# Cross attention with an adapter on one core: the adapter's sums over its heads as additions of halves, and the last rows stored in halves of columns

## The chip, the cores and the metric

The kernel runs on one core of a Trainium2 chip, everything in float32. The metric is the device time of one execution in microseconds (us). Five engines work beside each other: TensorE (PE, matrix products), VectorE (DVE), ScalarE (ACT), GpSimd (POOL) and SyncE (SP, which issues most of the DMAs, in order). Each has its own queue of instructions, and semaphores join them.

## The reference, cut to what matters

Two sequences of 2048 rows with 640 features attend to 124 text tokens, in 8 heads of 80. The last 4 tokens of the context feed an adapter: it forms 384 queries from them, attends with these to the 2048 rows of the sequence, multiplies by `Wq`, and attends again to its own 4 tokens. The 384 result rows are spread over the 2048 rows by an index, added to the text attention, and the sum goes through `Wout`.

```python
hs = _mha(query, keyt, valt)                     # text attention
ca_q1 = jnp.einsum('btc,th->bch', ca, Wq_ca)     # 384 adapter queries
ca_q1 = ca_q1[:, indices, :]                     # read for 2048 rows
ca_hs1 = _mha(ca_q1, residual, residual)         # attention to the rows of x
ca_hs2 = _mha(ca_hs1 @ Wq, ca @ Wk_ca, ca @ Wv_ca)
out = (hs + ca_hs2) @ Wout + b_out + residual
```

## The kernel before

The kernel is not one loop. Python generators describe pieces of work (`adapter`, `softmax`, `text_out_fast`, ...), each yields a `Do` for an engine with what it waits for, and a planner (`Desk`) simulates the engines: it adds up estimated durations (`desk.spent`) and issues next what is ready first, by rank among equals. The order found so is the program's order on each engine. L236 (VectorE, ScalarE and GpSimd work), L211 (products), L221 (transposes) and L256 (DMAs by SP) are the helpers through which all instructions go, so a profile names them all by these lines and the tiles tell them apart.

The adapter works on each sequence (batch `b`) in turn. Its weighted sums over the rows of x are never formed with 640 features; products with the keys of its second attention are carried along in their place. `contract(b, j, acc, at)` adds them up on PE in `acc` for two halves `j` of the eight heads, turns the result (`pt_acc`) and divides it, on DVE, into the tile `prod`. `prod` has shape (128 partitions, 3 groups of adapter queries, 2 halves `j`, 4 heads `g` in a half, 24), and the 24 are 8 heads of the second attention by 3 differences of tokens. `second(b)` then sums over the 8 heads of the first attention (`j` and `g`) into the scores `s2f`, in the function `less`, which goes on to take the maximum and subtract it. An exponential on ACT follows, `share` divides on DVE into `p2pad`, PE turns it (`pt_p`), and products with `w2_sb` give 384 rows that go to DRAM (`o`). From there `add_second` gathers rows on POOL by the index `query` and adds them to rows of output, by indirect DMAs.

The text attention goes in 16 units of two tiles of 128 rows. For unit `m`, `text_out_fast` takes probabilities that were turned by way of DRAM (`kept`, then `pT`), forms the heads' output (`ph`, `hs`), and multiplies by `Wout` in four chains with seven products for eight blocks; each chain's partial sum in PSUM (`po`) is added on DVE to a quarter of the output, half of a tile's 640 columns, in the residual's rows (`x_more` or `last_rows`, two sets of four row tiles). Each tile `(m, i)` receives four such additions, counted in `tile_left`; at the fourth `stored(m, i, ...)` issues the store on SP. In all units but the last, and there too if `o` were late, the gather comes between additions and store (`gather_last`); in the last it is done ahead of the additions.

The end of a chain's step, before:

```python
tile_left[m, i] = tile_left.get((m, i), 4) - 1
ends.setdefault((m, i), []).append(op.at)
if not tile_left[m, i]:
    yield Fork(stored(m, i, ends[m, i]), 1)
```

Of the kernel before, what the change touches and what calls it, by code (L numbers as in the profile page):

```python
# [11 lines left out]
ALU = mybir.AluOpType  # L12
AX = mybir.AxisListType

P = 128
# [49 lines left out]
class Desk:  # L65
# [188 lines left out]
    def dma(self, out, in_, us, issue=0.45, more=2.8):  # L254

        self.pin(self.nc.sync.dma_start(out, in_))  # L256
        self.spent += issue
        self.channel = max(self.channel, self.now + self.spent) + us
        self.landed = self.channel + more
# [3 lines left out]
def kernel(  # L263
# [20 lines left out]
    NCC = CAD // P  # L284
    NST = S // P
    NSB = S // 512
    HALF = H // 2
    SCALE = float(D) ** -0.5
    NUM, DEN = CAD - 1, S - 1
    T1 = T - 1  # L290
# [8 lines left out]
    UNITS = B * NST // 2  # L299
# [4 lines left out]
    desk = Desk(tc)  # L304
    matmul, transpose, copy, dma = desk.matmul, desk.transpose, desk.copy, desk.dma
# [13 lines left out]
    ending, late = Room(1), {}  # L319
# [47 lines left out]
    s2f = const.tile([P, NCC, HEADS, T], F32, name="s2f")  # L367
# [37 lines left out]
    for name, bands in (  # L405
# [4 lines left out]
        for n, (pattern, width, base, factor) in enumerate(bands):  # L410
            m = const.tile([P] + [k for _, k in pattern], F32, name=f"band_{name}_{n}")
# [1273 lines left out]
    def second(b):  # L1685

        def clear():
            desk.g_memset(p2pad, 0.0)
            desk.g_memset(p2pad[:, :, N2 : N2 + 1], 1.0)

        op = yield Do("POOL", clear, [])
        cleared = op.at
        N = NCC * HEADS
        s2 = s2f.rearrange("p a h t -> p (a h) t")
        p2 = small.tile([P, N, T], F32, tag="p2", name=f"p2_{b}", bufs=1)
        r2 = small.tile([P, N], F32, tag="r2", name=f"r2_{b}", bufs=1)

        def less():
            for ct in range(NCC):
                desk.v_tensor_reduce(  # L1700
                    s2f[:, ct, :, 1:],
                    late["prod"][:, ct, :, :, :].rearrange("p j g (h t) -> p h t (j g)", t=T1),
                    AX.X, ALU.add,
                )
            m2 = small.tile([P, N], F32, tag="m2", name=f"m2_{b}", bufs=1)
            desk.v_tensor_reduce(m2, s2, AX.X, ALU.max)
            desk.v_tensor_tensor(p2, s2, m2.unsqueeze(2).to_broadcast([P, N, T]), ALU.subtract)

        yield Do("DVE", less, [("prod", b, 0), ("prod", b, 1)])
        yield Do("ACT", lambda: desk.a_activation(p2, p2, AF.Exp, scale=SCALE))  # L1710

        def share():
            desk.v_tensor_reduce(r2, p2, AX.X, ALU.add)
            desk.v_reciprocal(r2, r2)
            p2of = p2.rearrange("p (a g j) t -> p a g j t", a=NCC, j=2)
            r2of = r2.rearrange("p (a g j x) -> p a g j x", a=NCC, j=2, x=1)
            for j in range(2):
                k0 = 2 * T * b + T * j
                desk.v_tensor_tensor(
                    p2pad[:, :, : 4 * G].rearrange("p a (g k) -> p a g k", g=4)[:, :, :, k0 : k0 + T],  # L1720
                    p2of[:, :, :, j, :], r2of[:, :, :, j, :].to_broadcast([P, NCC, 4, T]), ALU.mult,
                )

        op = yield Do("DVE", share)

        def turn(s):
            pt = bank(s[0], f"pt_p2_{b}")
            for ct in range(NCC):
                transpose(pt[: N2 + 1, ct * P : (ct + 1) * P], p2pad[:, ct, : N2 + 1], ident)
            return pt  # L1730

        op = yield Do("PE", turn, [op.at, cleared], needs=[(banks, 1)])
        pt, s = op.value, op.slots[0][0]

        def out_of(e):
            t = ea_tile(e[0], f"p2T_{b}")[: N2 + 1, 0, :]
            copy(t, pt[: N2 + 1, :CAD])
            return t

        op = yield Do("ACT", out_of, needs=[(eas, 1)], frees=[(banks, s)])  # L1740
        p2T, i = op.value, op.slots[0][0]
        here = op.at
        o2_of[b] = hbm.tile([CAD, H], F32, tag=f"o2_{b}", name=f"o2_{b}")
        for ct in range(NCC):
            op = yield Do("NONE", lambda e: ea_tile(e[0], f"o2_{b}_{ct}"), [here], needs=[(eas, 1)])
            o2, k = op.value.rearrange("p g k -> p (g k)")[:, :H], op.slots[0][0]
            for u in range(2):
                cols = slice(u * HALF, (u + 1) * HALF)

                def product(s, u=u, cols=cols):  # L1750
                    po = bank(s[0], f"po2_{b}_{ct}_{u}")
                    matmul(
                        po[:, :HALF], p2T[:, ct * P : (ct + 1) * P], w2_sb[:, cols],
                        start=True, stop=True,
                    )
                    return po

                op = yield Do("PE", product, [here, ("w2", u)], needs=[(banks, 1)])
                op = yield Do(
                    "ACT", lambda po=op.value, cols=cols: copy(o2[:, cols], po[:, :HALF]),  # L1760
                    frees=[(banks, op.slots[0][0])], marks=[("o2 part", b, ct, u)],
                )
            yield Do(
                "SP", lambda: dma(o2_of[b][ct * P : (ct + 1) * P, :], o2, 1.3),
                [("o2 part", b, ct, 0), ("o2 part", b, ct, 1)], frees=[(eas, k)],
                marks=[("o2 out", b, ct)],
            )
        yield Do(
            "NONE", lambda: None, [("o2 out", b, ct) for ct in range(NCC)], frees=[(eas, i)],
            marks=[("o2", b)],  # L1770
        )
        if b == B - 1:

            def more():
                sq_stack.close()
                late["ps"] = ctx.enter_context(tc.tile_pool(name="ps_r", bufs=1, space=bass.MemoryType.PSUM))
                banks.at += [desk.now] * 4
                ending.at += [desk.now] * 3

            yield Do("NONE", more, [])  # L1780
# [6 lines left out]
    kept_of, xr_of, gather_last, scored = {}, {}, {}, {}  # L1787

    def tiles(m):

        b, m = divmod(m, NST // 2)
        return [(b, 2 * m + k) for k in range(2)]
# [254 lines left out]
    def text_out_fast(m, rank):  # L2047
# [3 lines left out]
        for c0, n in ((0, 2), (2, 2), (4, 1)):  # L2051

            def product(s, z=None, c0=c0, n=n):
# [4 lines left out]
            op = yield Do(  # L2058
                "PE", product, [("pT", m), "v done"], needs=[(banks, 1)] + ([(hss, 1)] if c0 == 0 else []),
                frees=[(pTs, room_of["pT", m])] if c0 == 4 else [],  # L2060
                mode=(P, 32), rank=rank,
            )
# [9 lines left out]
        a = [[hs[:, 2 * k : 2 * k + 2, i * P : (i + 1) * P] for k in range(2)] for i in range(2)]  # L2072
# [29 lines left out]
        def chain(n, steps):  # L2102

            po, s, at = None, None, []
            for k, ((x, y, plus), after, ((i, u),)) in enumerate(steps):

                def product(s=None, k=k, x=x, y=y, plus=plus):
                    to = bank(s[0], f"po_{m}_{n}") if s else po
                    pairs = [(x[:, c], y[:, c]) for c in range(2)] if x is not None else []
                    if plus:  # L2110
                        pairs.append((last[plus[0]], five[plus[1]]))
                    for c, (l, r) in enumerate(pairs):
                        matmul(
                            to[:, :HALF], l, r, start=(k == 0 and c == 0), stop=(c == len(pairs) - 1),
                            skip_group_check=True,
                        )
                    return to

                op = yield Do(
                    "PE", product, after + at + ready, needs=[(banks, 1)] if k == 0 else [], mode=(P, P), rank=rank  # L2120
                )
                if k == 0:
                    po, s = op.value, op.slots[0][0]
                end = k == len(steps) - 1
                if end:
                    left["products"] -= 1
                    if not left["products"]:
                        hss.at[at_hs] = op.at.t

                def add(i=i, u=u, po=po):  # L2130
                    t = xr_of[m][i][0][:, u * HALF : (u + 1) * HALF]
                    desk.v_tensor_tensor(t, t, po[:, :HALF], ALU.add)

                op = yield Do("DVE", add, [op.at], frees=[(banks, s)] if end else [], rank=1)
                at = [op.at]
                tile_left[m, i] = tile_left.get((m, i), 4) - 1
                ends.setdefault((m, i), []).append(op.at)
                if not tile_left[m, i]:
                    yield Fork(stored(m, i, ends[m, i]), 1)
# [1 line left out]
        for n, steps in enumerate(chains):  # L2141
            yield Fork(chain(n, steps), 30 + m)

    fast_of, tile_left, ends = {}, {}, {}

    def added(m, k, u, po, s, at):

# [107 lines left out]
```

## Time and profile before

| what | us |
|---|---|
| median of three runs | 602.8 |
| lowest and highest | 601.7, 605.3 |
| profiled execution, its own time | 600.98 |
| span in its profile | 599.3 |
| reductions to `s2f`, first of batch 0 and of batch 1, start | 285.67, 476.77 |
| last addition on DVE, start | 594.92 |

The span runs from the first to the last instruction, the own time also holds what lies around it. Times in the profile are counted from the span's start. The page gives each engine's busy time, the chain of work that ended last, and the costliest groups of instructions. A row of the timeline gives start, duration, engine, helper line, operation, the tile written and those read with their shapes, and in brackets how long the engine had been idle and what ended that. The granted TensorE clock is full (1.000) throughout.

### The profile page before, as it was taken

The numbers are of one execution on the slowest core, as the hardware profiler recorded it, in microseconds if no ns is written. First come the engines' busy times: TensorE is split into PE (matmuls) and PEld (weight loads), VectorE is DVE, ScalarE is ACT, GpSimd is POOL, SyncE is SP. The second block draws the span as 40 slices with busy tenths as digits, with TensorE's granted clock in tenths as the row PEclk, the third lists the DMA queues.
The fourth block names the chain that finished last, engine by engine and source line by source line (L and its number), as shares of the span: only waits on it lengthen the run. The fifth ranks groups of instructions, "written<-read, shape, count | busy, mean of one in ns | idle before, by whom it ended". The sixth has DMA issues, their size and how long they took to land.

```text
span 599.3 us, 11936 instructions
## 1 busy us (share of the span) xinstructions
PE 583.7 (97%) x4535; PEld 363.9 (61%) x4535; DVE 390.8 (65%) x629; ACT 323.2 (54%) x913; POOL 133.4 (22%) x195
## 2 busy tenths in 40 slices
PE   9999999999999999999999999999999999999997
PEld 6475456567756655555665666555555567666664
DVE  2257789899999485445989999845532443444343
ACT  2233345865688789898757776478767420101010
POOL 7211122124002430010006231243022122413241
PEclk9999999999999999999999999999999999999999
DMA  8998956784958584543899898986643977899986
GB/s 268 173 248 127 181 128 199 142 226 137 187 172 179 146 164 126 170 124 110 193 269 272 209 225 251 237 188 189 179 124 67 249 152 205 204 232 254 224 197 166
DMA packets 152244, 112.25 MB, mean 187 GB/s; under 512 B 83190, under 2 KB 125558, under 8 KB 152187
## 3 DMA queue, kind: packets, MB, share of 16 engines
q1 hardware_dynamic: 146554, 100.80, 66.7%
q0 software_dynamic: 5632, 10.69, 10.7%
q8 instruction: 36, 0.59, 0.4%
q14 instruction: 22, 0.17, 0.1%
HBM read 71.23 MB, written 40.22 MB: 186 GB/s over the span
## 4 chain that ended last, share of the span: by engine, by line
PE 60%; DVE 18%; DMA 9%; ACT 7%; issue 4%; SPq 1%; ACTq 0%; DVEq 0%
PE po L211 20%; PE pq L211 16%; DVE mx L236 7%; PE acc L211 5%; PE ph L211 5%; PE s L211 4%; DMA pT<-kept 4%; ACT p L236 3%; PE sc L211 3%; ACT ea L236 3%; PE pyz L211 3%; DVE m L236 2%; DVE eb L236 2%; DMA kept<-eb 2%; DMA out_dram<-x_more 1%
## 5 line engine op out<-in xcount | busy, mean ns | idle before, releaser
L236 DVE TENSOR_REDUCE mx<-s 128x4 f32<-128x2048 f32 x48 | 109.4, 2279 | 7.7 <-PE s L211 7.5
L236 ACT ACTIVATE ea<-s 128x2048 f32<-128x2048 f32 x48 | 90.8, 1892 | 23.2 <-PE s L211 20.3
L236 ACT ACTIVATE p<-sc,m 128x124 f32<-128x124 f32 x256 | 90.0, 379 | 10.1 <-DVE m L236 10.0
L211 PE MATMUL pq<-xt,wq_sb 128*128 128x256 f32 (+1 forms) x272 | 86.1, 452 | 0.2
L211 PE MATMUL po<-wout_sums,hs 128*128 128x320 f32 x256 | 78.3, 439 | 0.3 <-ACT p L236 0.3
L211 PE MATMUL po<-wout_sb,hs 128*128 128x320 f32 x232 | 72.8, 441 | 0.0
L211 PEld LDWEIGHTS pq<-xt,wq_sb 128*128 128x128 f32 x272 | 48.9, 190 | 25.6 <-issue 17.0
L236 ACT COPY hs<-ph 128x512 f32<-128x512 f32 (+1 forms) x31 | 17.5, 570 | 84.5 <-PE ph L211 84.4
L211 PEld LDWEIGHTS po<-wout_sums,hs 128*128 128x128 f32 x256 | 47.1, 190 | 24.4 <-issue 4.5
L236 DVE TENSOR_TENSOR x_more<-x_more,po 128x320 f32<-128x320 f32 x64 | 30.8, 484 | 44.3 <-PE po L211 43.7
L236 ACT ACTIVATION_READ_ACCUMULATOR p<-sc,m 128x1 f32 x256 | 56.6, 221 | 0.0
L236 DVE TENSOR_TENSOR last_rows<-last_rows,po 128x320 f32<-128x320 f32 x64 | 30.8, 483 | 38.0 <-PE po L211 37.6
L211 PEld LDWEIGHTS po<-wout_sb,hs 128*128 128x128 f32 x232 | 42.4, 190 | 21.2 <-ACT hs L236 2.5
L236 ACT ACTIVATE p<-p,r 128x124 f32<-128x124 f32 x144 | 43.7, 389 | 18.1 <-DVE r L236 18.1
L211 PE MATMUL acc<-ea,y_sb 128*32 128x384 f32 (+2 forms) x768 | 51.4, 385 | 0.0
L236 DVE TENSOR_REDUCE m<-sc 128x4 f32<-128x496 f32 x64 | 40.7, 667 | 15.5 <-PE sc L211 15.5
L211 PE MATMUL ph<-pT,vpad 128*32 128x256 f32 x768 | 46.5, 381 | 3.0 <-DMA pT<-kept 2.3
L2005 POOL DMA_INDIRECT x_more<-o,query x16 | 24.9, 1555 | 92.7 <-DVE x_more L236 59.6
L236 DVE STREAM_TRANSPOSE eb<-p 128x1024 f32<-128x1024 f32 x32 | 39.6, 1237 | 1.9 <-ACT p L236 1.4
L2005 POOL DMA_INDIRECT last_rows<-o,query x16 | 24.8, 1548 | 71.1 <-DVE last_rows L236 64.8
L211 PE MATMUL pq<-xt,wq 128*128 128x512 f32 x80 | 39.5, 612 | 0.0
L211 PEld LDWEIGHTS sc<-kmain,q 64*128 64x128 f32 x512 | 31.3, 187 | 12.2 <-issue 9.9
(208 smaller groups left out, 812.5 us busy)
## 6 DMA issues: line engine op xcount, KB each, us to landing
kept<-eb SPq DMA_DIRECT2D x32, 512.0 KB
pT<-kept SPq DMA_DIRECT2D x64, 256.0 KB
landing<-away SPq DMA_DIRECT2D x60, 128.0 KB
xi<-in_x_dram SPq DMA_DIRECT2D x28, 256.0 KB
x_more<-in_x_dram SPq DMA_DIRECT2D x16, 320.0 KB
last_rows<-in_x_dram SPq DMA_DIRECT2D x16, 320.0 KB
out_dram<-x_more SPq DMA_DIRECT2D x16, 320.0 KB
out_dram<-last_rows SPq DMA_DIRECT2D x16, 320.0 KB
```

Of the source, the lines that this page charges most:

```text
L211: self.pin(self.nc.tensor.matmul(out, lhsT, rhs, **kw))
L236: self.pin(getattr(engine, what)(*args, **kw))
L2005: desk.pin(nc.gpsimd.indirect_dma_start(out=t, out_offset=None, in_=o2_of[b], in_offset=bass.IndirectOffsetOnAxis(ap=query[:, st : st + 1] ...
```

## The change

Two places. In `less`, the three strided reductions (one for each group of adapter queries, 192 elements a row to 24) give way to three additions: the halves `j` are added in place (288 elements a row: 3 x 4 x 24), then heads 2 and 3 of the four onto 0 and 1 (144), then the last two into `s2f` (72). A constant is added to the planner's estimate, so that `less` is as long for the planner as before (0.704 + 0.075 against 0.779 us), and the order of the instructions on each engine stays. In the last unit, when its gather is ahead of the additions, each column half of a tile is stored by itself when its two additions are done.

```diff
         def less():
-            for ct in range(NCC):
-                desk.v_tensor_reduce(
-                    s2f[:, ct, :, 1:],
-                    late["prod"][:, ct, :, :, :].rearrange("p j g (h t) -> p h t (j g)", t=T1),
-                    AX.X, ALU.add,
-                )
+            prod = late["prod"]
+            desk.v_tensor_tensor(prod[:, :, 0], prod[:, :, 0], prod[:, :, 1], ALU.add)
+            desk.v_tensor_tensor(prod[:, :, 0, :2], prod[:, :, 0, :2], prod[:, :, 0, 2:], ALU.add)
+            desk.v_tensor_tensor(
+                s2f[:, :, :, 1:], prod[:, :, 0, 0].rearrange("p a (h t) -> p a h t", t=T1),
+                prod[:, :, 0, 1].rearrange("p a (h t) -> p a h t", t=T1), ALU.add,
+            )
+            desk.spent += 0.07488
...
                 at = [op.at]
+                if m == UNITS - 1 and not gather_last[m]:
+                    half_ends.setdefault((i, u), []).append(op.at)
+                    if len(half_ends[i, u]) == 2:
+                        yield Fork(stored_half(m, i, u), 1)
+                    continue
                 tile_left[m, i] = tile_left.get((m, i), 4) - 1
...
+    def stored_half(m, i, u):
+
+        b, st = tiles(m)[i]
+        cols = slice(u * HALF, (u + 1) * HALF)
+        t = xr_of[m][i][0]
+        yield Do("SP", lambda: dma(out[b, st * P : (st + 1) * P, cols], t[:, cols], 0.7), half_ends[i, u])
```

On SP the stores at the end were, in order, four of `x_more` and two of `last_rows` (128 x 640). They are now one of `x_more`, one half of `last_rows` (128 x 320), three of `x_more`, and three halves of `last_rows`.

More of the change, by code (lines that the diff above doesn't have):

```diff
@@ L2142, in text_out_fast @@
             yield Fork(chain(n, steps), 30 + m)
-    fast_of, tile_left, ends = {}, {}, {}
+    fast_of, tile_left, ends, half_ends = {}, {}, {}, {}
+    def stored_half(m, i, u):
[3 more added lines that the diff above has]
+        yield Do("SP", lambda: dma(out[b, st * P : (st + 1) * P, cols], t[:, cols], 0.7), half_ends[i, u])
     def added(m, k, u, po, s, at):
```

## The prediction

> **What bounds the kernel now.** I read the page's busy shares first, then the chain that ended last, then stretches of 20 us, then the waits.
>
> ```profile
> PE 583.7 (97%) x4535; PEld 363.9 (61%) x4535; DVE 390.8 (65%) x629; ACT 323.2 (54%) x913; POOL 133.4 (22%) x195
> PE 60%; DVE 18%; DMA 9%; ACT 7%; issue 4%; SPq 1%; ACTq 0%; DVEq 0%
> 280.00:300.00 20.00, 18.53 (x135) 13.31 (x134) 19.13 (x29) 13.58 (x53) 0.00 (x0) 1.00 0.73 177
> 300.00:320.00 20.00, 19.59 (x106) 13.39 (x104) 17.63 (x17) 11.58 (x45) 0.98 (x1) 1.00 1.07 282
> 360.00:380.00 20.00, 19.67 (x138) 11.84 (x138) 20.00 (x23) 11.97 (x50) 4.96 (x5) 1.00 0.80 233
> 440.00:460.00 20.00, 20.00 (x217) 10.20 (x219) 4.01 (x9) 13.71 (x9) 4.61 (x3) 1.00 0.37 78
> 500.00:600.00 100.00, 94.88 (x578) 63.33 (x576) 40.88 (x87) 9.85 (x20) 27.87 (x18) 1.00 0.88 211
> PE pt_p L221 <- DVE p2pad L236: 1.5, 1, 1.5
> PE ph L211 <- DMA pT<-kept: 2.3, 3, 1.3
> ```
>
> PE is busy 97% of the span, so a saving on another engine counts only where PE waits for it. The columns of a stretch are its length, then busy time of PE, PEld, DVE, ACT and POOL with counts, the granted clock (1.00), the DMA share and GB/s. Around 280 to 380 us DVE is as full as PE (19.13 and 20.00 of 20); from 440 on DVE is mostly idle and PE sets the pace. The last two rows are PE's waits: in 287 to 386 us its longest is 1.5 us, for `p2pad`, which DVE writes at the end of the adapter's first softmax; in 386 to 477 us it waits 2.3 us in three pieces for `pT`. The change works ahead of that 1.5 us wait, ahead of its twin at 480 us, and at the end.
>
> **The adapter's sums, batch 0.** The order of instructions on every engine stays as it was, but for the three reductions, which become three additions at the same place on DVE.
>
> ```profile
> 285.67 1.67 DVE L236 TENSOR_REDUCE s2f<-prod 128x24 f32<-128x192 f32 x3
> 286.88 1.89 PE L211 MATMUL pq<-xt,wq_sb 128*128 128x256 f32 x8
> 286.95 0.60 ACT L236 CAST zop<-zb 128x512 fp32r<-128x512 f32 x1
> 287.37 0.25 DVE L236 TENSOR_REDUCE m<-s2f 128x24 f32<-128x96 f32 x1
> 287.95 0.28 ACT L236 ACTIVATE p<-p 128x96 f32<-128x96 f32 x1 [0.39 <-DVE p L236]
> 289.08 0.25 DVE L236 TENSOR_REDUCE r<-p 128x24 f32<-128x96 f32 x1
> 290.24 0.55 PE L221 MATMUL pt_p<-ident,p2pad 128*113 128x128 f32 x3 [1.47 <-DVE p2pad L236]
> L236 DVE TENSOR_TENSOR prod<-pt_acc,r 128x288 f32<-128x288 f32 x4 | 1.8, 458 | 0.1
> L236 DVE TENSOR_TENSOR x_sums<-pq,x_sums 128x256 fp32r<-128x256 f32 x7 | 2.9, 416 | 3.2 <-ACT x_sums L236 3.2
> L236 DVE TENSOR_TENSOR p<-s2f,m 128x96 f32<-128x96 f32 x2 | 0.5, 258 | 0.1
> L236 DVE TENSOR_TENSOR p2pad<-p,r 128x48 f32<-128x48 f32 x4 | 0.7, 206 | 0.1
> ```
>
> Before: from the first reduction's start, 285.67, to the start of `m` at 287.37 are 1.70 us. After: additions of 288, 144 and 72 elements a row. The trace has the first size, 0.458 us. Between 96 elements (0.258) and 256 (0.416) the slope is 0.99 ns an element, so 144 cost 0.258 + 48 x 0.99 ns = 0.305; between 48 (0.206) and 96 it is 1.08 ns, so 72 cost 0.232. Each addition reads what the one before it wrote, so their ends don't overlap, as those of the reductions do (3 x 0.613 is 1.84, drawn in 1.67); a step between dependent instructions costs about 0.03 (287.34 to 287.37 here). I take 0.04 three times. Sum 0.458 + 0.305 + 0.232 + 0.12 = 1.11, a saving of 0.59 us. Bounds: all three as short as the 48-element row, 3 x 0.206 + 0.12 = 0.74 (0.96 saved), or all as long as the 288-element one, 1.49 (0.21 saved).
>
> Does it reach PE? `m` then starts at 286.78, ACT's exponential could start at 287.36 but ACT is in its cast of `zop` until 286.95 + 0.60 = 287.55; it ends at 287.83 at the latest, long before `r` needs it, which moves with DVE's queue from 289.08 to 288.49. So `p2pad` and the transpose that PE waits for come 0.59 earlier, and PE had ended its product at 286.88 + 1.89 = 288.77, so all of it is taken from the 1.47 us wait. Behind it DVE's queue is full until 386, and it too starts 0.59 earlier. I take 0.59; the end below is 0, if a transfer holds the stretch (first rival).
>
> **Batch 1.**
>
> ```profile
> 476.77 1.68 DVE L236 TENSOR_REDUCE s2f<-prod 128x24 f32<-128x192 f32 x3
> 478.49 0.25 DVE L236 TENSOR_REDUCE m<-s2f 128x24 f32<-128x96 f32 x1
> 478.97 1.24 PE L211 MATMUL po<-wout_sb,hs 128*128 128x320 f32 x4
> 480.48 0.56 PE L221 MATMUL pt_p<-ident,p2pad 128*113 128x128 f32 x3 [0.27 <-DVE p2pad L236]
> ```
>
> The same additions take 1.11 in place of 478.49 - 476.77 = 1.72, but PE is in its own products until 478.97 + 1.24 = 480.21 and waits only 0.27. So 0.27 of the 0.61 count; bounds 0 and 0.27. From here PE runs without another wait of note, and so the end moves with it.
>
> **The last unit's stores.** The last unit has two tiles of 128 rows; each gets four additions on DVE, two to each half of its 640 columns. Before, a tile is stored when all four are done; after, each half when its two are. Two stores become four.
>
> ```profile
> 593.28 2.49 SPq L256 DMA_DIRECT2D out_dram<-last_rows  x2
> 594.92 0.49 DVE last_rows L236
> GB/s 0 269 384 397 384 205 0 0 0 0 141 410 397 410 282 0 0 0 0 0 0 269 384 397 384 205 0 0 0 0 0 0 0 0 41 0 0 0 0 0
> SPq L2250 <- DMA out_dram<-last_rows: 1.7, 1, 1.7
> q1 hardware_dynamic: 146554, 100.80, 66.7%
> ```
>
> The last addition ends at 594.92 + 0.49 = 595.41, and the last store is issued at once: the SP row ends at 595.77, its last issue is 0.33 of that. The throughput row has slices of 0.2 us from 592.0. The last store fills five of them from 596.2, in all about 0.84 us (328 KB at some 390 GB/s), the end of the queue waits 1.7 us for it, and what follows is the program's closing. That last store now carries half the bytes, in 128 pieces of 1,280 B rather than 2,560. If the time goes with the bytes, 0.42 is saved; if with the pieces, nothing. Between them: over the whole span a piece of the queue is 100.80 MB / 146,554 = 688 B and takes 0.667 x 599.3 x 16 / 146,554 = 43.6 ns; here eight pieces a DMA engine in 0.84 us make 105 ns. On a line through both, 1,280 B take 63 ns, eight of them 0.51 us. I take 0.84 - 0.51 = 0.33. The half ahead of it is complete when the addition before last ends, about 594.9, and is issued in 0.33, so SP is free at 595.43; its data (0.85 us after issue, as for the store before) pass at 595.75 to 596.26, just out of the way. If they did collide, the gain would be 0, no loss.
>
> **Sum.** 0.59 + 0.27 + 0.33 = 1.19 us. The profiled execution took 600.98 (span 599.3 and 1.68 around it), so 599.8 for its like. The median of the three runs is 602.8, 1.8 above that, with 601.7 to 605.3 as extremes; the forecast for it is 601.6. About 0.5%, 3 us, is what a measurement of this kernel tells from no change; 1.2 us lies inside.
>
> **Rivals.**
>
> ```profile
> L256 SPq DMA_DIRECT2D out_dram<-x_more x3: 332/332/333, 586.0 to 591.4; - x3
> 587.92 0.49 DVE L236 TENSOR_TENSOR last_rows<-last_rows,po 128x320 f32<-128x320 f32 x1 [1.13 <-PE po L211]
> 584.62 1.55 POOL L2005 DMA_INDIRECT x_more<-o,query  x1 [0.30 <-DVE hs L236]
> L236 DVE TENSOR_TENSOR x_sums<-xt 128x512 f32<-128x512 f32 x1 | 1.3, 1283 | 0.0
> L236 DVE TENSOR_TENSOR x_sums<-xt,x_sums 128x512 f32<-128x512 f32 x4 | 2.7, 676 | 0.0
> 210.38 1.27 POOL L236 TENSOR_TENSOR x_sums<-xt 128x512 f32<-128x512 f32 x1 [8.28 <-DVE xt L236]
> 319.02 3.05 POOL L236 TENSOR_TENSOR wout_sums<-wout_sb 128x640 f32<-128x640 f32 x2 [61.65 <-PE pq L211]
> 473.30 0.73 POOL L236 TENSOR_TENSOR hs<-hs 128x256 f32<-128x256 f32 x1 [6.25 <-ACT hs L236]
> 487.78 1.54 POOL L2005 DMA_INDIRECT last_rows<-o,query  x1 [13.74 <-DVE last_rows L236]
> ```
>
> (a) The DMA engines take batch 0's gain: 300 to 320 us show a share of 1.07, so transfers that leave DVE 0.59 earlier may arrive when they did. For it: the full share there. Against: the share is 0.73 just before, and DVE's own queue needs no transfer for most of its work. Then 0.60 is left: 602.2.
>
> (b) The half store is as long as the whole: 0.86 is left, 601.9.
>
> (c) Faster than the sum: batch 0's earlier stores to `kept` end the 2.3 us of waits for `pT`, which are released by transfers and not by PE. For it: they come as pieces of 1.3 us and less. Against: PE comes there earlier as well. 1.19 + 2.3 = 3.5 us: 599.3.
>
> (d) Slower: the first finished half is queued on SP ahead of three stores of `x_more`. It is ready at 587.92 + 0.49 = 588.41, but the first of those stores went at 586.0, so this one is held to 588.7, and 328 + 164 KB then leave beside the last gather (issued 584.62), for which the store at 591.4 waits. The last half is late only if that store slips by more than 595.43 - 591.76 - 2 x 0.33 = 3.0 us; the bytes moved are worth 492 KB / 390 GB/s = 1.3 us. If the slip were two of the present spacings of these stores (591.4 - 586.0 = 5.4), the end comes 2.4 later: +1.2 net, 604.0. To be 0.5% slower it needs 7.2.
>
> (e) The additions run at about double length, as one addition of two SBUF operands did at 210.9 us (1.283 against 0.676) while POOL added beside it (210.38 to 211.65). Three at +0.46, +0.31 and +0.23 would be 0.41 longer than the reductions, and the sum would be +0.41 + 0.41 - 0.33, about 0.5 us slower, 603.3. Against it: POOL has nothing for 61.65 us up to 319.02, and between 474.03 and 487.78, so neither place has an overlap. [...]
>
> **How the numbers follow.** Chances: forecast 0.55, (a) 0.17, (b) 0.08, (c) 0.09, (d) 0.06, (e) 0.01, and 0.04 for shifted transfers whose place I can't name. Only (c) passes 3 us on the fast side: 0.09. Slower by 0.5% is the far end of (d), 0.01, and the unnamed, 0.04. The range runs from (c), 599.2 with its rounding, to (d) with a little of the runs' scatter, 604.2.
>
> **What would show it.** In the profile after: the three additions at 0.46, 0.31 and 0.23 us with `m` 1.1 us behind the first one's start; PE's wait for `p2pad` at 0.9 rather than 1.47 and none at 480; everything near 480 some 0.6 earlier; four stores of 160 KB, the last filling about 0.5 us. It is wrong if PE's wait shrinks but the work at 386 us starts no earlier (a), if the last `x_more` store goes after 594.4 (d), or if the additions take over 1.5 us.

## The result, and the profile after

| | before | after |
|---|---|---|
| median of 18 runs each, us | 602.61 | 600.38 |
| lowest and highest | 600.95, 605.74 | 598.56, 601.77 |
| profiled execution, own time | 600.98 | 600.67 |
| its span | 599.3 | 599.0 |

The ratio after to before is 0.9958, with a 95% interval of 0.9943 to 0.9973: 2.2 us less at the median, where 1.2 were forecast. The two profiled executions differ by 0.3 us only. Executions of one kernel are 3 to 5 us apart, so two profiles can't be compared by their ends; they can be compared piece by piece, since most pieces repeat to 0.03 us. The first row is from the page of after, then its timeline around the sums of batch 0, the transpose that PE waits for, and the same for batch 1.

```profile
PE 583.9 (97%) x4535; PEld 364.9 (61%) x4535; DVE 389.5 (65%) x629; ACT 323.4 (54%) x913; POOL 133.6 (22%) x195
...
286.21 0.79 DVE L236 TENSOR_TENSOR prod<-prod 128x288 f32<-128x288 f32 x2
287.03 0.23 DVE L236 TENSOR_TENSOR s2f<-prod 128x72 f32<-128x72 f32 x1
287.30 0.25 DVE L236 TENSOR_REDUCE m<-s2f 128x24 f32<-128x96 f32 x1
...
290.17 0.55 PE L221 MATMUL pt_p<-ident,p2pad 128*113 128x128 f32 x3 [0.85 <-DVE p2pad L236]
...
476.35 0.49 PE L221 MATMUL pt_acc<-ident,accs 128*128 128x128 f32 x3
...
477.71 0.80 DVE L236 TENSOR_TENSOR prod<-prod 128x288 f32<-128x288 f32 x2
478.54 0.23 DVE L236 TENSOR_TENSOR s2f<-prod 128x72 f32<-128x72 f32 x1
478.81 0.25 DVE L236 TENSOR_REDUCE m<-s2f 128x24 f32<-128x96 f32 x1
...
480.99 0.49 PE L221 MATMUL pt_p<-ident,p2pad 128*113 128x128 f32 x3
...
481.31 1.24 PE L211 MATMUL po<-wout_sb,hs 128*128 128x320 f32 x4
```

From the first instruction of the sums to `m` are 1.09 us (286.21 to 287.30) where the reductions took 1.70, and to PE's transpose 3.96 where it was 4.57. PE's wait for `p2pad` has shrunk from 1.47 to 0.85 us in batch 0, and in batch 1 the row of the transpose names no wait any more.

```profile
588.86 0.33 SPq L256 DMA_DIRECT2D out_dram<-last_rows  x1
589.25 2.52 SPq L256 DMA_DIRECT2D out_dram<-x_more  x3
593.71 2.49 SPq L256 DMA_DIRECT2D out_dram<-last_rows  x3
594.81 1.03 DVE L236 TENSOR_TENSOR last_rows<-last_rows,po 128x320 f32<-128x320 f32 x2 [1.13 <-PE po L211]
GB/s 0 0 26 269 371 384 333 218 180 346 384 371 282 197 0 0 0 0 0 0 0 0 0 0 0 0 0 0 0 0 0 0 0 0 0 0 0 0 0 0
SPq L2264 <- DMA out_dram<-last_rows: 1.1, 2, 0.6
```

At the end the last addition is done at 594.81 + 1.03 = 595.84 and the span ends at 599.0: a tail of 3.16 us, against 599.3 - 595.41 = 3.89 before. The throughput row has slices of 0.1 us from the last issue, 595.87; two halves pass behind each other, the second from about 0.8 to 1.4 us after the last issue began.

That gives six pieces that can be followed through all profiles: the way to the sums (285.67 to 286.21 us in these eight, not in the table), the sums to the transpose in batch 0, the stretch from there to `pt_acc` in batch 1, from `pt_acc` to the product behind the transpose in batch 1, the rest to the last addition, the tail.

| profile | sums to transpose, b. 0 | stretch to batch 1 | `pt_acc` to product, b. 1 | to last addition | tail |
|---|---|---|---|---|---|
| before | 4.57 | 185.17 | 5.46 | 114.54 | 3.89 |
| after | 3.96 | 186.18 | 4.96 | 114.53 | 3.16 |
| both_again | 3.97 | 184.25 | 4.97 | 114.52 | 3.18 |
| both_third | 3.96 | 187.67 | 4.96 | 114.52 | 3.13 |
| sums_only | 3.96 | 184.52 | 4.96 | 114.53 | 3.88 |
| halves_only | 4.57 | 188.11 | 5.45 | 114.53 | 3.05 |
| sums_b0 | 3.97 | 187.90 | 5.45 | 114.54 | 3.91 |
| sums_b1 | 4.57 | 185.58 | 4.97 | 114.51 | 3.89 |

Local savings, then: 0.61 + 0.50 + 0.73 = 1.84 us. In every profile of the table that holds the part the sums' savings are the same to 0.02 us, the tail's to about 0.1 (tails of 3.05 to 3.18 us). Nearly all that scatters lies in one piece, the stretch between the two batches, 184.3 to 188.1 us.

Batch 0's saving can be followed into that stretch. Two of DVE's transposes of probabilities there, in before and then in after:

```profile
335.57 1.24 DVE L236 STREAM_TRANSPOSE eb<-p 128x1024 f32<-128x1024 f32 x1
383.71 1.24 DVE L236 STREAM_TRANSPOSE eb<-p 128x1024 f32<-128x1024 f32 x1
...
335.35 1.24 DVE L236 STREAM_TRANSPOSE eb<-p 128x1024 f32<-128x1024 f32 x1
383.54 1.24 DVE L236 STREAM_TRANSPOSE eb<-p 128x1024 f32<-128x1024 f32 x1
```

Counted from the sums' first instruction, they start after 49.90 and 98.04 us before, and after 49.14 and 97.33 with the change. The first lies at 49.90 to 50.58 us in the five profiles with the three reductions in batch 0 (before, halves_only, sums_b1, fill_403, fill_b0), mean 50.13, and at 49.14 to 49.59 in seven with the additions (after, both_again, both_third, sums_only, sums_b0, both_fill, quarters), mean 49.40. The second lies at 97.77 to 98.74 (mean 98.16) and 96.98 to 98.15 (mean 97.61). So the saving is whole 50 us on, and 0.55 us are left of it in the mean at 384 us, where the ranges overlap. Behind that the profiles part by over 3 us, at a wait around 403 us (below).

### The profile page after: what moved, and what is told of

Its sections match the earlier page's. It is cut to its first block, busy times and chain, and to the rows that moved or that the text cites. A ratio compares the mean times of both kernels' runs of the same rounds, so it can differ in the third digit from the quotient of the medians.

```text
span 599.0 us, 11938 instructions
## 1 busy us (share of the span) xinstructions
PE 583.9 (97%) x4535; PEld 364.9 (61%) x4535; DVE 389.5 (65%) x629; ACT 323.4 (54%) x913; POOL 133.6 (22%) x195
## 4 chain that ended last, share of the span: by engine, by line
PE 65%; DVE 14%; DMA 11%; ACT 6%; issue 2%; SPq 1%; ACTq 0%; DVEq 0%
PE po L211 23%; PE pq L211 16%; DMA pT<-kept 8%; PE ph L211 6%; DVE mx L236 5%; PE acc L211 5%; PE s L211 4%; PE sc L211 3%; ACT p L236 3%; PE pyz L211 3%; ACT ea L236 2%; DVE m L236 2%; SPq L256 1%; DVE eb L236 1%; PE pv L211 1%
```

## Experiments

**One part alone, and both again.** sums_only is the kernel before with the three additions of the changed one, its first hunk:

```diff
-            for ct in range(NCC):
-                desk.v_tensor_reduce(
...
+            prod = late["prod"]
+            desk.v_tensor_tensor(prod[:, :, 0], prod[:, :, 0], prod[:, :, 1], ALU.add)
...
```

halves_only is the kernel before with the other hunks:

```diff
+                if m == UNITS - 1 and not gather_last[m]:
+                    half_ends.setdefault((i, u), []).append(op.at)
...
+    def stored_half(m, i, u):
...
```

both_again is the changed kernel itself. The theories differ in what reaches the end.

> The changed kernel as it is, beside the runs that do one part alone, on the same chip. All theories: about 2.2 us faster than before (0.996). For the tail, from the end of the last addition on DVE to the end of the span: 3.2 us, as in the first profile of it, against 3.9 before; for the way from the first instruction of the sums to the start of the transpose on PE: 3.96 in batch 0 (4.57 before), 3.3 in batch 1 (3.7 before). If these differ by more than 0.1 from the first profile, one profile is not enough to size a term.

> Only the additions in place of the reductions; stores as before. Theory 1 (the savings are local and all reach the end): the two local savings, 0.61 and 0.43, give 1.0 us, so 0.9983 of before; tail 3.9. Theory 2 (rival c: batch 0's earlier stores also end some of PE's waits for pT): 1.5 to 3 us, 0.995 to 0.9975. Theory 3 (rival a: batch 0's gain is eaten by transfers, the stores do the rest): 0.3 to 0.4 us, above 0.9990.

> Only the last unit's stores in halves; reductions as before. Theory 1: 0.7 us, the difference of the two tails (3.89 and 3.16), 0.9988 of before. Prediction's own size of this term: 0.33 us, 0.9995. Theory 3: 1.5 to 2 us, 0.997. All: PE's waits for p2pad as before, 1.5 and 0.3; tail 3.2.

Measured beside 24 runs of before (mean 602.03): both_again 0.9951 (0.9935 to 0.9968), 3.3 us in the mean of 7 runs; sums alone 0.9980 (0.9964 to 0.9996), 1.6 us; halves alone 0.9986 (0.9969 to 1.0003), 0.6 us. The parts' local times are those of the table. Sums and halves alone fit theory 1 (1.0 and 0.7), with intervals of some 0.9 us either way; both together came out over it. Theory 3, in which the stores do most, expected 0.997 from the halves and above 0.9990 from the sums; the sums' interval ends at 0.9996 and doesn't exclude that by itself.

**More of the reductions in batch 0** (more_b0). The kernel before, with its three reductions made three times in batch 0.

```diff
         def less():
+            if b == 0:
+                at = desk.spent
+                for _ in range(2):
+                    for ct in range(NCC):
+                        desk.v_tensor_reduce(
+                            s2f[:, ct, :, 1:],
+                            late["prod"][:, ct, :, :, :].rearrange("p j g (h t) -> p h t (j g)", t=T1),
+                            AX.X, ALU.add,
+                        )
+                desk.spent = at
```

> The kernel before, with batch 0's three reductions made three times over (six more on DVE, some 0.54 us each as they overlap, 3.2 us in all), the planner's estimate unchanged. Theory 1 and 2: the stretch is bound by DVE and all of the 3.2 us reaches the end, 1.005 of before (1.0045 to 1.0060). Theory 3: transfers set the pace behind it, and 1 us or less arrives, below 1.002.

1.0074 (1.0056 to 1.0092), 4.0 us in the mean of 6 runs, above the 3.2 put in. From the sums to the transpose are 7.74 us, 3.17 more. A row of its timeline and three windows (the third number from the end is the granted clock):

```profile
293.57 0.96 PE L221 MATMUL pt_p<-ident,p2pad 128*113 128x128 f32 x3 [4.63 <-DVE p2pad L236]
285.00:290.00 5.00, 3.94 (x20) 2.96 (x16) 5.00 (x10) 2.71 (x9) 0.00 (x0) 1.00 0.84 161
290.00:295.00 5.00, 1.43 (x5) 1.37 (x6) 4.79 (x12) 3.27 (x16) 0.00 (x0) 0.66 0.23 79
295.00:300.00 5.00, 5.00 (x18) 3.52 (x17) 3.65 (x4) 2.12 (x8) 0.00 (x0) 0.66 0.77 197
```

Transfers don't swallow the delay, as theory 3 and rival (a) would have it: the second of the two transposes above starts here 102.95 us after the sums' first instruction, 4.8 us later than in the mean of the five profiles with three reductions. Of this 3.17 us were put in. The rest goes with the clock. The wait of 4.63 us is followed by a granted clock of 0.66 in two windows of 5 us, and the transpose of three tiles takes 0.96 instead of 0.55. Taken as either 1.00 or 0.50, the clock is at 0.50 for 3.4 us in each of the two windows, and for 4.4 in that from 291 to 296 (0.56): one stretch from 291.6, 2.6 us after the end of PE's last product, to 298.4. DVE's `eb<-p` that starts at 299.29 us in before starts at 304.30 here, 4.85 us later when both are counted from the sums. All six executions have a mean clock of 0.993 or 0.994, so the 4.0 us hold this cost too.

**Where executions differ: the wait around 403 us.** In the stretch that scatters, PE waits for `pT`, which comes back from DRAM. In three profiles the clock falls at the end of that wait or just behind it, by the windows from some 0.1 us ahead of the end to 0.7 behind. Of halves_only and both_third, the waiting product and the windows of 2 us (granted clock third from the end):

```profile
404.58 1.28 PE L211 MATMUL ph<-pT,vpad 128*32 128x256 f32 x16 [2.09 <-DMA pT<-kept]
404.00:406.00 2.00, 1.42 (x17) 0.70 (x18) 0.08 (x1) 1.30 (x1) 0.00 (x0) 0.83 1.07 183
406.00:408.00 2.00, 2.00 (x4) 1.31 (x5) 1.21 (x3) 0.00 (x0) 1.20 (x1) 0.50 1.01 339
408.00:410.00 2.00, 2.00 (x13) 1.07 (x11) 0.32 (x1) 0.00 (x0) 1.86 (x2) 0.82 0.10 36
```

```profile
404.52 1.93 PE L211 MATMUL ph<-pT,vpad 128*32 128x256 f32 x16 [1.88 <-DMA pT<-kept]
404.00:406.00 2.00, 1.48 (x16) 0.68 (x16) 0.00 (x0) 1.44 (x1) 0.00 (x0) 0.59 1.01 182
406.00:408.00 2.00, 2.00 (x11) 1.14 (x5) 0.94 (x3) 0.00 (x0) 0.60 (x1) 0.56 1.03 324
408.00:410.00 2.00, 2.00 (x18) 1.19 (x20) 0.84 (x3) 0.00 (x0) 1.85 (x2) 1.00 0.16 58
```

The third is sums_b0 (wait 2.00, clock 0.91 from 400 to 405 us and 0.75 from 405 to 410). Taken as either 1.00 or 0.50 again, the clock is at 0.50 for 3.4 us in each of the three, which by estimate, half of that, costs PE some 1.7 us of work. These are the three longest stretches of the table, 187.7 to 188.1, and the executions are the slowest or nearly so of their kernels (603.55 of at most 603.62, 601.83, 603.29). In the others of the table the wait was 1.27 to 1.69 us and the clock stayed at 1.00. The runs also give the mean clock of each execution, profiled or not. It is 0.996 or 0.997 in these three, and 0.997 or less in 24 of the 80 executions of before that were measured beside the experiments; these took 603.0 us in the mean, the other 56 took 601.1. (In after the clock also falls in the last microseconds, when PE has no work left, to 0.79 from 597 to 598 us and 0.50 from 598 to 599; with 1.00 up to 590 that alone makes its mean 0.999.) So about half of the 4 us between executions goes with the clock.

From here on three theories are told apart. L: the local savings are all. G: the lowered clock behind batch 0's wait of 1.47 us is part of the gain. P: the lowered clock behind the wait around 403 us is what differs. fill_403 puts four products of the identity, whose result nothing uses, into that last wait; the trace counts them as eight.

```diff
-                return hidden(m, c0, n, bank(s[0], f"ph_{m}_{c0}"))
+                ph = bank(s[0], f"ph_{m}_{c0}")
+                if c0 == 0:
+                    begun_c0.append(m)
+                    if len(begun_c0) == 6:
...
+                        for _ in range(4):
+                            matmul(ph[:, :P], ident, ident, start=True, stop=True)
...
+                return hidden(m, c0, n, ph)
```

> The kernel before, with four such products ahead of the product that waits for pT around 403 us (1.3 to 2.1 us in six profiles; after the wait of 2.1 the granted clock was 0.5 for about 4 us). Theory P: executions above 603 us are those in which that wait lowered the clock; they go, the mean falls by 0.5 to 0.8 us and the spread from about 4 to below 3 us. Theories G and L: no change, 1.000 plus or minus 0.0015, the same spread.

> The changed kernel with the products ahead of the wait for pT around 403 us: a version that may beat both. Theory P: 0.5 us below the changed kernel, 0.9945 of before. G and L: as the changed kernel, 0.9955.

Before with these products: 0.9983 (0.9971 to 0.9996), 0.6 us in the mean, and the highest of 12 runs is 602.15, where 8 of the 27 runs of before beside it lie above 602.2. None of the 22 executions with the products, 12 on before and 10 on the changed kernel (both_fill), has a mean clock under 0.998. The wait that is left is 0.97 us:

```profile
402.80 1.16 PE L211 MATMUL ph<-ident 128*128 128x128 f32 x8
404.93 1.07 PE L211 MATMUL ph<-pT,vpad 128*32 128x256 f32 x16 [0.97 <-DMA pT<-kept]
```

So work that nobody needs, 1.16 us of it, makes the kernel faster, as theory P had it: with products in that wait no execution shows the lowered clock. Batch 0's wait is still there in that profile (1.46 us), which speaks against theory G. On the changed kernel the products brought nothing that shows: 0.9965 (0.9950 to 0.9980), against 0.9951, 0.9958 and 0.9978 without, but the changed kernel without them was not measured beside it. fill_403 was: between these two, neither of which shows the lowered clock, the change is worth 601.00 - 599.57 = 1.4 us in the mean, some 0.8 us either way.

**The same ahead of batch 0's transpose** (fill_b0).

```diff
             pt = bank(s[0], f"pt_p2_{b}")
+            if b == 0:
...
+                for _ in range(4):
+                    matmul(pt[:, :P], ident, ident, start=True, stop=True)
```

> The kernel before, with four products of the identity on PE (about 1 us) in the bank of the adapter's transpose of batch 0, ahead of its wait for p2pad, so that PE idles some 0.5 instead of 1.5 us there; nothing waits for them. It asks where the sums' gain beyond the local 1.1 us comes from. Theory G (in some executions PE's wait of 1.47 us lowers the granted clock for some microseconds, as the wait of 4.63 us did with more reductions; the additions end that): the mean falls by 0.5 to 1 us, 0.9985 to 0.9990 of before, with the sums still slow. Theory L (the local savings are all; what is beyond is scatter) and theory P (the gain lies in the waits for pT around 403 us): 1.000 plus or minus 0.0015.

1.0024 (1.0009 to 1.0039), slower. The experiment missed its aim. Its rows on PE show why; two windows stand behind them:

```profile
290.10 1.16 PE L211 MATMUL pt_p<-ident 128*128 128x128 f32 x8 [0.90 <-ACT p L236]
291.09 0.49 PE L221 MATMUL pt_p<-ident,p2pad 128*113 128x128 f32 x3
...
404.09 1.07 PE L211 MATMUL ph<-pT,vpad 128*32 128x256 f32 x16 [2.10 <-DMA pT<-kept]
404.00:406.00 2.00, 1.91 (x19) 1.17 (x20) 0.78 (x3) 0.79 (x1) 0.00 (x0) 1.00 1.05 240
406.00:408.00 2.00, 2.00 (x18) 1.19 (x20) 0.87 (x4) 0.00 (x0) 1.85 (x1) 1.00 0.69 241
```

The bank was free only when ACT had read the scores in it, at 290.1, so the products ran behind the wait and made the transpose 0.42 us later (4.99 for 4.57). Theory G is thus not tested by it. Nor is the 0.42 us on the path: DVE's `eb<-p` near 336 us starts 50.05 us after the sums, within the 49.90 to 50.58 of the other profiles with reductions. Why the kernel took 1.3 us more in the mean stays open. This one profile does show that the stretch behind batch 0 follows DVE's queue and not PE's transpose. The last rows are worth keeping: here a wait of 2.10 us left the clock at 1.00, while 1.88 lowered it in both_third. The length alone doesn't decide; what else does, no run here shows.

**The sums split by batch.** The edit of sums_b0, on the kernel before; sums_b1 has `b == 1` in its first line. both_third is the changed kernel.

```diff
         def less():
+            if b == 0:
+                prod = late["prod"]
+                desk.v_tensor_tensor(prod[:, :, 0], prod[:, :, 0], prod[:, :, 1], ALU.add)
...
+            else:
                 for ct in range(NCC):
                     desk.v_tensor_reduce(
...
```

> The changed kernel once more, on the chip of the two runs that split the sums. Local savings by five profiles: 0.61 in batch 0, 0.50 in batch 1, 0.72 at the end, 1.83 in all. Theory L (nothing beyond these): 0.9970 of before. Theory S (an earlier batch 0 also shortens the stretch behind it, up to batch 1, by some 0.6 us in the mean): 0.9960.

> Additions in batch 0 alone, reductions in batch 1, whole stores. Both theories: from the first instruction of the sums to the transpose 3.96 us in batch 0, 3.7 in batch 1, tail 3.9. Theory L: 0.61 us faster, 0.9990. Theory S: 1.2 us, 0.9980.

> Additions in batch 1 alone. Both theories: 4.57 us in batch 0, 3.3 in batch 1, tail 3.9, and 0.50 us faster, 0.9992, with the spread of the kernel before. If it gains over 1 us, the gain beyond the local savings doesn't hang on batch 0.

Beside 29 runs of before: both_third 0.9978 (0.9962 to 0.9993), 1.3 us in the mean; batch 0 alone 0.9993 (0.9978 to 1.0008), 0.2 us; batch 1 alone 0.9997 (0.9980 to 1.0014), 0.25 us. Theory S, an extra gain behind batch 0, expected 1.2 us of sums_b0 and is not borne out, though its 0.9980 lies just inside the interval. Both parts lie below their local 0.61 and 0.50, by less than the intervals' 0.9 us; by themselves these two runs show neither saving. Over the three comparisons the whole change gave 2.4, 3.3 and 1.3 us in the mean, some 2.3 together, each with an interval of about 0.9 us either way; the local 1.84 is in reach of it. A gain beyond the local savings is not shown.

**The last half in quarters.** The changed kernel with the last tile's second half in two stores of 160 columns.

```diff
-        yield Do("SP", lambda: dma(out[b, st * P : (st + 1) * P, cols], t[:, cols], 0.7), half_ends[i, u])
+        for k in range(2 if (i, u) == (1, 1) else 1):
+            n = HALF // 2 if (i, u) == (1, 1) else HALF
+            cols = slice(u * HALF + k * n, u * HALF + (k + 1) * n)
+            yield Do("SP", lambda: dma(out[b, st * P : (st + 1) * P, cols], t[:, cols], 0.7 / (1 + k)), half_ends[i, u])
```

> The changed kernel with the very last half of 128 x 320 stored in two quarters of 160 columns, both issued on SP when it is complete. It asks what the 0.7 us at the end hang on, of which the data explain 0.37. If the time between last byte and the closing goes with the size of the last transfer: the data start 0.3 later for the second quarter and the tail stays at 3.2 us or falls to 3.0. If each DMA has its own price in it: 3.4 to 3.5 us. Local times of the sums: 3.96 and 3.28 us as before.

One execution, 598.44. Its SP row and the end of its additions:

```profile
591.24 2.98 SPq L256 DMA_DIRECT2D out_dram<-last_rows  x4
592.34 1.02 DVE L236 TENSOR_TENSOR last_rows<-last_rows,po 128x320 f32<-128x320 f32 x2 [1.13 <-PE po L211]
```

The tail is 596.7 - 593.36 = 3.34, between the two forecasts and 0.2 longer than with halves, since SP takes 0.33 for one more issue. From the last issue (594.22 - 0.33 = 593.89) to the end are 2.81 us; it is 3.02 to 3.16 in the profiles with 160 KB and 3.82 to 3.89 in those with 320 KB. So the end goes with the size of the last transfer, by about 0.73 us from 320 to 160 KB and 0.32 from 160 to 80, some 1.5 to 1.7 times what the bytes need at 390 GB/s. The 80 KB are one profile, and as the rows stay 128, the bytes of a row shrink with the size; the runs don't part the two.

**POOL beside the additions.** Six products of 192 elements a row, behind DVE's reciprocal `r`, in the changed kernel.

```diff
+        if j:
+            beside = small.tile([P, NCC, 4, 16], F32, tag="beside", name=f"beside_{b}", bufs=1)
+            w = wout_sb[:, 0, :192].rearrange("p (a g k) -> p a g k", a=NCC, g=4)
+
+            def besides():
+                for _ in range(6):
+                    desk.g_tensor_tensor(beside, w, r.unsqueeze(3).to_broadcast([P, NCC, 4, 16]), ALU.mult)
+                desk.spent = 0.0
+
+            yield Do("POOL", besides)
```

> The changed kernel with six multiplications of 192 elements a row on POOL, which start when DVE's reciprocal is done and run beside the additions, in both batches; nothing uses their result. Rival (e) as a mechanism: the additions that overlap with them take about double, 0.8 to 0.9 in place of 0.46 us for the first. Without it (two SBUF operands on DVE don't meet POOL's reads): 0.46, 0.31 and 0.23 us as before.

```profile
285.13 3.56 POOL L236 TENSOR_TENSOR beside<-wout_sb,r 128x192 f32<-128x192 f32 x6 [27.37 <-DVE r L236]
286.04 1.04 DVE L236 TENSOR_TENSOR prod<-prod 128x288 f32<-128x288 f32 x2
287.12 0.48 DVE L236 TENSOR_TENSOR s2f<-prod 128x72 f32<-128x72 f32 x1
L236 DVE TENSOR_TENSOR prod<-prod x4: 458/500/508, 286.0 to 476.8; 128x288 f32<-128x288 f32 x2, 128x144 f32<-128x144 f32 x2
L236 POOL TENSOR_TENSOR beside<-wout_sb,r x12: 511/512/686, 285.1 to 479.0; 128x192 f32<-128x192 f32 x12
```

The loss that rival (e) names shows, in another form than expected: the first addition didn't double, but five of the six took 0.48 to 0.51 us, near the 0.51 of one instruction of POOL (0.48 for the smallest, which needs 0.23 alone), and the sixth its own 0.458. The way from sums to transpose was 4.49 us, 0.53 longer than alone and all but the 4.57 of the reductions; in batch 1 it was 5.32 us from `pt_acc` to the product, against 4.96 without POOL and 5.46 with the reductions. With these products of POOL beside it, the exchange is worth next to nothing, 0.08 us in batch 0 and 0.14 in batch 1. Why the additions are longer there, no row tells.

## Why the prediction was right

**The reading of the bound** held, with one shift. The saving on DVE in batch 0 goes on behind it (0.73 us at 336 us, 0.55 in the mean at 384), and a delay there does too (more_b0). But it travels in DVE's full queue, which the prediction named second; PE's wait, which it named first, only shows it, for in fill_b0 the transpose came 0.42 us later and DVE's work at 336 us did not.

**Batch 0.** Forecast: 0.458 + 0.305 + 0.232 with three steps, 1.11 us in place of 1.70, 0.59 saved. Measured: 0.459, 0.307 and 0.234, 1.09, and 0.61 saved at PE. The cover that was named, PE's wait, gave 0.62 of its 1.47.

**Batch 1** was mis-sized: 0.27 forecast as the most it could be, 0.50 measured from `pt_acc` to the product behind the transpose. The step that failed is that a removed wait gives back its own length. Before, the product ahead ended, PE stood still, the transpose began at 480.48 and the next product 0.39 later. After, the transpose begins at 480.99, ahead of the modelled end of the row before it (479.91 + 1.24 = 481.15), and the next product 0.32 later. Without the wait the instructions overlap, 0.2 us more than the wait's row shows.

**The end** was mis-sized most: 0.33 forecast, 0.73 measured. The data's own share was right to the width of the slices: the last bytes passed 1.7 to 1.75 us after their issue and now 1.38, 0.32 to 0.37 less. But I took what follows the data for fixed, and it shrank too, by 0.36 to 0.41. The quarters fit that it goes with the transfer's size. What it consists of, no row tells. One time in that part is misread: 594.9 + 0.33 makes SP free at 595.23 and not at 595.43; nothing hangs on it, since the last half is complete only at 595.41.

**The rivals.** (a) had the sign that the work at 386 us starts no earlier; counted from the sums it starts 0.55 us earlier in the mean at 384, and in more_b0 a delay arrived there. The other sign, all near 480 us some 0.6 earlier, can't be read in one profile: in after `pt_acc` came 0.94 us later (476.35 for 475.41), as that stretch scatters by more. (b) fell with the throughput row. (c): PE's waits for `pT` were 2.3 us in before, and 3.5, 1.8 and 2.8 in profiles of after, so they scatter and don't go; but it is there that the executions differ. (d): the half went out at 588.86 and the last store of `x_more` was issued by 589.25 + 2.52 = 591.77, where it had been 591.76; no slip at all. (e) needs POOL at work, which it isn't at either place, and the additions took their own time; pool_beside shows what it would cost.

**The sum.** 1.19 forecast, 1.84 by the local pieces, 2.2 by the medians of the first comparison (1.3 to 3.3 by the means of three): the two mis-sized terms are 0.23 and 0.40 of the difference, the rest is within what the executions scatter. That the median, 600.38 for 601.6, fell into a range of 5 us checks none of the terms; the pieces do. 0.2 us of that distance is the start: before has 602.61 as the median of 18 where 602.8 was that of three. And the 3 us named as what a measurement can tell were too wide: the interval of 18 runs each is 0.9 us either way.

## What to carry to other kernels

Cut the profiles of two kernels into pieces at events that both have, and compare piece by piece: here three pieces repeat to 0.03 us and the tail to about 0.1, and one of 185 us holds nearly all of the scatter. Where the last instruction is a store, as here, see what halving the last transfer gives: it gave 0.73 us, where 160 KB at 390 GB/s are 0.42. Before a VectorE reduction is exchanged for additions of two SBUF operands, look at what GpSimd does at that place: with six of its products beside the additions, 0.08 us of batch 0's 0.61 were left here.

## What was not expected of the hardware

PE's wait around 403 us cost nearly as much again in three profiles: after 1.88, 2.00 and 2.09 us (both_third, sums_b0, halves_only) the granted clock was at 0.50 for 3.4 us, by estimate some 1.7 us of work. After 1.27 to 1.69 us it stayed at 1.00, and after 2.10 in fill_b0 too. Four unneeded products in that wait made the kernel before 0.17% faster (0.04 to 0.29%). And the time from the last issue of a store to the end of the program was about 3.86 us for 320 KB (before), 3.13 for 160 KB (after) and 2.8 for 80 KB (quarters).
